# Holding back and interleaving PSUM drains in a two-layer attention kernel

## The chip, the cores and the metric

The kernel runs on one core of one Trainium2 chip. The metric is the device time of one execution in microseconds (us), less is better. The engines are called PE (TensorE, matrix products into PSUM), DVE (VectorE), ACT (ScalarE), POOL (GpSimd) and SP (SyncE, whose queue issues the DMAs).

## What is computed

Two attention layers, one after the other, on eight independent images (elements) of 512 channels and 32 x 32 = 1024 positions, all in fp32:

```python
# layer 0 (8 heads of 64 channels)
hn = group_norm(x, gn1_scale, gn1_bias)                     # 32 groups
q, k, v = split(einsum('bchw,oc->bohw', hn, w_qkv) + b_qkv) # per head
wgt = softmax(einsum('bct,bcs->bts', q * s, k * s))
a = einsum('bts,bcs->bct', wgt, v)
out = einsum('bchw,oc->bohw', a, w_proj) + b_proj
x = x + group_norm(out, gn2_scale, gn2_bias)
# layer 1 (one head of 512 channels; the rows of w_qkv, w_out are weight-normed)
qkv = einsum('oc,bcn->bon', w_qkv, x);  qkv = qkv / rms(qkv)
attn = softmax(einsum('bci,bcj->bij', q, k) * C ** -0.5)
h = einsum('oc,bcn->bon', w_out, einsum('bij,bcj->bci', attn, v))
x = (x + h) * 2 ** -0.5
```

## The kernel before

**Order.** Every instruction is issued through `InOrder` (line 34 is its call, so the profile names line 34 for nearly everything, and tiles tell the work apart). Each engine runs its instructions in program order; waits between engines are semaphores that the framework sets from the tiles' readers and writers. The order is written out by hand: generators (`steps`, `pieces`) issue a little work at each `next`.

**An element's layer 0** is a loop of 64 steps (`Heads.step`, 606): scores for 128 rows and two heads (`s`), softmax with its maximum on DVE (`nm`), exponential on ACT, scaling on POOL (`p<-p,tt`), a DVE transpose (`pb<-p`) in `turn` (560), four DMAs that lay the result out (`pT<-pb`), and for every second step 32 matmul passes with the values (`po<-pT,v`, `values`, 585). In the last eight steps POOL also forms the sums of the next element's input that the next stage needs (`tv`, lines 1242 on, one sum a step).

**Products in sevens.** `Seven` (715) computes a product of 2 x 2 blocks with seven products instead of eight. Their operands on one side are called B11, T2, T3, T4, T1, B22, B21, in this order; T1 to T4 are sums of blocks (`RightSide`, 678). Each product is two matmuls, which the trace shows as four passes. Two successive products share one PSUM tile (`product`, 730), whose name ends in B or T after its first product. A product's result is added into the outputs by small functions, the *drains*: `c11_first` (a copy on ACT), then sums on DVE (T2's into c12, T3's into c22, `c21`, `both` with two sums, `c12`, `c11`). They are put in a list, and the whole list is issued as soon as a tile has both its products (`Seven.drain`, 749). The tiles come from a pool of three (`wide`, 110; `ps_s`), which the scores share; a fourth tile waits until the first one is emptied.

**The hand-over from layer 0 to layer 1** (from line 1251, seven times: the last element has another ending, `finish_last`, 647). PE's work, in order:

- four products of the next element's values (`project_v7`, 517; profile names `p_v_B`, `p_v_T`). There are four units of seven products, 28 in all, one unit after the other;
- `values` for the last group but one (1255); then `heads.turn()` (1256) issues the last transpose and its DMAs; SP fetches the output projection's weights (`proj7`, profile name `proj`) and layer 1's norm matrix (`gram`);
- DVE forms five sums of the attention's output (`ta`), PE computes ten more products of the values;
- `values` for the last group (1271); the loads of `x`, for which a slot must be free, are queued on SP;
- `finish_layer0` (799): two units of seven products for the output projection (`p_o_B`, `p_o_T`) into `o`, whose statistics DVE takes (`bn_stats`, `bn_aggr`). Then the last fourteen products of the values are spread over the second group norm: four; `norm.means()` (PE's `pm`, then on DVE the mean, and `d`); two; `norm.coeffs()` (PE's `pv`, then `ve`, a Newton iteration for the inverse root in `rsqrt_steps`, 195, and the coefficients `a` and `c`); then four times two products, ACT's `o<-o,c,a` and DVE's `x<-x,o` for one of the four channel blocks;
- `Layer1.project` (865): `py`, the product of `x` with `gram`. The tile for channel block cj needs `x` up to block cj. DVE multiplies it with `x` and forms the sums `t` for the following sevens.

Of the kernel before, what the change touches and what calls it, by code (L numbers as in the profile page):

```python
# [10 lines left out]
AF = mybir.ActivationFunctionType  # L11
ALU = mybir.AluOpType
# [40 lines left out]
def attention_blocks_kernel(  # L53
# [29 lines left out]
    CI, NT, HN = C // P, N // P, N // 2  # L83
# [20 lines left out]
    PE, VE, AC, PO, SY = (InOrder(tc, e) for e in (nc.tensor, nc.vector, nc.scalar, nc.gpsimd, nc.sync))  # L104

    def big(name, lead=CI):

        return slots.take([P, lead, CI * N // lead], name)

    def wide(name):  # L110
        return ps_s.tile([P, 2, HN], F32, tag="sc", name=name)
# [11 lines left out]
    def run(pieces):  # L123
        for _ in pieces:
            pass
# [24 lines left out]
    def load_x(b, xt, ci):  # L150
        SY.dma_start(out=xt[:, ci, :], in_=xv[b, :, ci, :])
# [40 lines left out]
    def col(base, i):  # L192
        return cols[:, base + i : base + i + 1]

    def rsqrt_steps(r, v, n, name):

        t = small.tile([P, 4 * CI], F32, tag="rs_t", name=f"rs_{name}")[:, :n]
        VE.tensor_scalar(r.bitcast(I32), v.bitcast(I32), -0.5, 1597463007.0, ALU.mult, ALU.add)
        yield
        for _ in range(3):  # L200
            VE.tensor_mul(t, r, v)
            VE.tensor_mul(t, t, r)
            VE.tensor_scalar(t, t, -0.5, 1.5, ALU.mult, ALU.add)
            VE.tensor_mul(r, r, t)
            yield

    def rsqrt(r, v, n, name):
# [22 lines left out]
    def place(name, b):  # L230
        tag, shape = places[name]
        near[name] = weights.tile(shape, F32, tag=f"w_{tag}", name=f"{name}_{b}")
        if name == "v":

            near["v7"] = near[name]
            flat = near[name].rearrange("p k h c -> p (k h c)")
            near["v#"], near["v_"] = flat[:, CI * C :], flat[:, : CI * C]
            near[name] = flat[:, : CI * C].rearrange("p (ci c) -> p ci c", ci=CI)
        return near[name]
# [13 lines left out]
    def fetch(name, b):  # L253
        SY.dma_start(out=place(name, b), in_=far[name])
# [16 lines left out]
    def gn_stats(st, src, k):  # L271
        VE.bn_stats(st[:, k, :], src[:, k * HN : (k + 1) * HN])

    class GroupNorm:
# [8 lines left out]
        def mean_steps(self):  # L283
            mv, n = self.mv, self.n
            pm = self.bank(f"pm_{self.name}")
            PE.matmul(pm[:, :n], gavg, mv[:, :, 0], start=True, stop=True)
            yield

            self.mean, self.d = self.new("mean"), self.new("d")
            VE.tensor_copy(self.mean, pm[:, :n])  # L290
            VE.tensor_sub(self.d, mv[:, :, 0], self.mean)
            VE.tensor_mul(self.d, self.d, self.d)
            VE.tensor_add(self.d, self.d, mv[:, :, 1])

        def means(self):
            run(self.mean_steps())
# [121 lines left out]
    class Sums:  # L418
# [32 lines left out]
        def right(self, half, n, k):  # L451

            rows = halves[half]
            if n == 0 or (n, half) in ((1, 0), (3, 1)):
                return self.hn[rows, k, HN:] if n == 0 else self.hn[rows, k, :HN]
            return (self.t24 if n + half == 2 else self.t3)[rows, k]
# [60 lines left out]
    def project_v7(b, right, v):  # L517

        w = near["v7"]
        for m in range(CI):  # L520
            c = {f"{i + 1}{th + 1}": v[:, m + 4 * th, i * CH : (i + 1) * CH] for i in range(2) for th in range(2)}
            yield from Seven(
                f"v0_{b}_{m}", CH,
                lambda k, h: w[:, k, h, :], right(slice(m * P, (m + 1) * P)), c, lambda which: None, swap=True,
            ).steps()

    class Heads:
        def __init__(self, b, hn, v, qk):
# [186 lines left out]
    class Seven:  # L715
# [5 lines left out]

        half, drains = None, []

        def __init__(self, name, width, left, right, c, last, swap=False, bias=None):
            self.name, self.width, self.left, self.right, self.swap = name, width, left, right, swap
# [2 lines left out]
        def product(self, a, b, drain):  # L730
            first = Seven.half is None
            if first:
                tile_ = wide(f"p7_{self.name}_{b}")
                pm, Seven.half = tile_[:, 0], tile_[:, 1]
            else:
                pm, Seven.half = Seven.half, None
            pm = pm[:, : self.width]
            for h in range(2):
                l, r = self.left(a, h), self.right(b, h)
                if self.swap:  # L740
                    l, r = r, l
                PE.matmul(pm, l, r, start=(h == 0), stop=(h == 1))

            Seven.drains.append(lambda: drain(pm))
            if not first:
                Seven.drain()

        @staticmethod
        def drain():
            for f in Seven.drains:  # L750
                f()
            Seven.drains = []

        def steps(self):
            c, add, last = self.c, VE.tensor_add, self.last
# [43 lines left out]
    def finish_layer0(b, h, rhs, xt, v0):  # L799

        o, w = big(f"o_{b}"), near["proj7"]
        st = small.tile([P, CI, 2, 6], F32, tag="gn_st2", name=f"st2_{b}")
        mv = small.tile([P, CI, 2], F32, tag="gn_mv2", name=f"mv2_{b}")
        norm = GroupNorm(mv, CI, G2S, G2B, f"2_{b}")

        def unit(m):
            c = {
                f"{i + 1}{th + 1}": o[:, m + 2 * i, th * HN : (th + 1) * HN] for i in range(2) for th in range(2)
            }
            return Seven(  # L810
                f"o_{b}_{m}", HN,
                lambda k, hh: w[:, k, hh, m * P : (m + 1) * P], rhs.columns(slice(0, HN)), c, lambda which: None,
                bias=(col(BP, m), bpd[:, m : m + 1]),
            ).steps()

        def stats(j):
            for k in range(2):
                gn_stats(st[:, j], o[:, j, :], k)

        units = [unit(m) for m in range(2)]  # L820
        for u in units:
            next(u)

        for j in range(CI // 2 + 1, CI):
            rhs.sums(j)
        for m, u in enumerate(units):
            for k in range(6):
                next(u)
                if k == 3:
                    stats(m + 2)  # L830
            stats(m)
        slots.give(f"a_{b}")
        slots.give(f"ta_{b}")
        fetch("score", b)

        def products(n):
            for _ in range(n):
                next(v0)

        for j in range(CI):  # L840
            VE.bn_aggr(mv[:, j, :], st[:, j])
        products(4)
        norm.means()
        products(2)
        a, c = norm.coeffs()
        for j in range(CI):
            products(2)
            AC.activation(o[:, j, :], o[:, j, :], AF.Identity, bias=c[:, j : j + 1], scale=a[:, j : j + 1])
            VE.tensor_add(xt[:, j, :], xt[:, j, :], o[:, j, :])
        run(v0)  # L850
        slots.give(f"tv_{b + 1}")
        slots.give(f"o_{b}")

    class Layer1:
# [163 lines left out]
        def products(self, th, c, between=None):  # L1018
            self.po = bank(f"po1_{self.b}_{th}_{c}")
            e = self.e[th]  # L1020

            terms = [(self.v[:, t, c * P : (c + 1) * P], e[:, t, :]) for t in (0, 4, 1, 5, 2, 6, 7, 3)]
            for k, _ in enumerate(matmuls(self.po, terms)):
                if k == 1 and between:
                    between()
# [16 lines left out]
    gram = place("gram", 0)  # L1042
# [64 lines left out]
    coeffs = norm1.gn.all_steps()  # L1107
# [64 lines left out]
    for b in range(B):  # L1172
        hn, more = heads.hn, b + 1 < B
        todo, due, rest = iter(()), [], []
        for i in range(STEPS):
            j, r = divmod(i, NB)
# [29 lines left out]
            if not b:  # L1206
# [10 lines left out]
                if k == 0:  # L1217
                    coeffs = norm1.gn.all_steps()
# [13 lines left out]
            m, odd = divmod(i - STEPS + NB, 2)  # L1232
# [11 lines left out]
            if not more and i == STEPS - 4:  # L1244
                xt = big(f"x_{b}")
# [4 lines left out]
        if more:  # L1250
            v0_next = big(f"v0_{b + 1}", NT)
            v0 = project_v7(b + 1, right_v.columns, v0_next)
            for _ in range(4):
                next(v0)
        heads.values(STEPS // RG - 2)
        heads.turn()
        if more:
            fetch("proj7", b)
            fetch("gram", b)
            ta = big(f"ta_{b}").rearrange("p (k i) (h n) -> p k i h n", k=2, h=2)  # L1260
            rhs = RightSide(heads.a, ta[:, 0], ta[:, 1])
            for j in range(CI // 2 + 1):
                rhs.sums(j)
            for _ in range(10):
                next(v0)
        else:
            fetch("score", b)
            begun = OutBegun(b, heads)
            for ci in (2, 3):
                load_x(b, xt, ci)  # L1270
        heads.values(STEPS // RG - 1)
        slots.give(f"v0_{b}")
        if more:
            xt = big(f"x_{b}")
            for ci in range(CI):
                load_x(b, xt, ci)
            finish_layer0(b, heads, rhs, xt, v0)
        else:
            finish_last(b, heads, xt, o_last, begun)
# [81 lines left out]
```

## Time and profile before

| | us |
|---|---|
| median of 3 runs | 3277.99 (3277.52 to 3279.08) |
| the profiled execution | 3280.76 |
| its span, first to last instruction | 3278.6 |
| PE busy | 3223.2 |
| DVE busy | 2304.4 |
| POOL busy | 1200.7 |
| ACT busy | 1046.7 |
| one hand-over, element 2: first of 28 products to first `py` | 1077.25 to 1137.97 |

The busy times are sums over all stages. PE's matmuls are pipelined and their ends are modelled: a 128 x 512 pass is listed with 592 ns and a 128 x 256 pass with 379 ns, while passes in a row start every 0.43 and 0.216 us. So a gap on PE is best read from starts. In the timeline a row is: start, duration, engine, line, operation, output<-inputs, shape, number of instructions merged, and in brackets the idle time before the row with what ended it. In a list of waits a row is: who waited, for whom, total us, how often, longest.

### The profile page before, as it was taken

Reading aid. Unit: us, or ns where it says so; the run is one execution under the profiler, and the core shown is the slowest. Engines: PE = TensorE matmul, PEld = TensorE weight load, DVE = VectorE, ACT = ScalarE, POOL = GpSimd, SP = SyncE. Lnnn points to the kernel's source line nnn. Section 1 sums busy time; section 2 is a strip of 40 time slices with the busy share of each in tenths; the row PEclk is TensorE's granted clock in tenths of the full one; section 3 lists DMA queues with packets and bytes.
Section 4 is the critical chain, followed back from the end, with each engine's and each line's share of the span. In section 5 each row is a group of like instructions: output and inputs, shape, how many; then the busy total and the mean of one; then the engine's idle time right before and its main releaser. Section 6 shows DMA issues by size and latency. Waiting matters only on the chain. (4 is left out here: it accounts for less than half of the span.)

```text
span 3278.6 us, 36790 instructions
## 1 busy us (share of the span) xinstructions
PE 3223.2 (98%) x13346; PEld 1661.9 (51%) x13346; DVE 2304.4 (70%) x3182; ACT 1046.7 (32%) x1813; POOL 1200.7 (37%) x1004
## 2 busy tenths in 40 slices
PE   8999999999999999999999999999999999999899
PEld 5455644455444554445544555445554456445354
DVE  5696667866678656886668866687667876568653
ACT  2453114521145111551215402254023531245210
POOL 1553124721257112670226603265023641246121
PEclk9999999999999999999999999999999999999899
DMA  6777215862168511783228822388224872158500
GB/s 199 212 202 205 74 48 154 221 186 58 48 180 229 167 42 54 201 230 133 52 77 211 213 108 52 101 213 244 71 57 109 216 213 74 23 153 212 180 7 26
DMA packets 231579, 447.34 MB, mean 136 GB/s; under 512 B 28996, under 2 KB 69480, under 8 KB 225512
## 3 DMA queue, kind: packets, MB, share of 16 engines
q1 hardware_dynamic: 231280, 444.97, 48.6%
q8 instruction: 107, 1.75, 0.2%
q14 instruction: 72, 0.59, 0.1%
q10 hardware_dynamic: 120, 0.02, 0.0%
HBM read 133.06 MB, written 29.52 MB: 50 GB/s over the span
## 5 line engine op out<-in xcount | busy, mean ns | idle before, releaser
L34 ACT ACTIVATE p<-s,nm 128x1024 f32<-128x1024 f32 x512 | 565.6, 1109 | 888.3 <-DVE nm L34 782.8
L34 POOL TENSOR_SCALAR p<-p,tt 128x1024 f32<-128x1024 f32 x512 | 566.0, 1118 | 754.3 <-DVE tt L34 750.4
L34 DVE TENSOR_REDUCE nm<-s 128x1 f32<-128x1024 f32 x512 | 601.7, 1216 | 151.4 <-PE s L34 151.0
L34 DVE STREAM_TRANSPOSE pb<-p 128x2048 f32<-128x2048 f32 x256 | 589.8, 2304 | 36.1 <-DMA pT<-pb 27.2
L34 PE MATMUL s<-qk 64*128 64x512 f32 x2048 | 527.6, 604 | 1.4 <-POOL qk L34 0.8
L34 PE MATMUL po<-pT,v 128*64 128x256 f32 x4096 | 471.8, 383 | 3.0 <-DMA pT<-pb 2.9
L34 PE MATMUL po<-e,v 128*128 128x512 f32 x1024 | 451.7, 595 | 0.0
L34 PEld LDWEIGHTS po<-pT,v 128*64 128x64 f32 x4096 | 284.6, 137 | 221.4 <-ACT v L34 31.8
L34 POOL TENSOR_TENSOR u<-u,xy 128x512 f32<-128x512 f32 x64 | 78.9, 1270 | 764.5 <-DVE u L34 392.3
L34 PEld LDWEIGHTS s<-qk 64*128 64x128 f32 x2048 | 201.9, 186 | 252.1 <-issue 225.2
L34 PEld LDWEIGHTS po<-e,v 128*128 128x128 f32 x1024 | 191.9, 190 | 245.0 <-issue 236.4
L34 PE MATMUL pq<-hn,qk 64*128 64x512 f32 x504 | 197.1, 592 | 0.0
L34 POOL TENSOR_TENSOR esum<-esum,e 128x512 f32<-128x512 f32 x96 | 130.5, 1361 | 154.2 <-ACT e L34 151.7
L34 ACT ACTIVATE e<-e,shift,rinv 128x512 f32<-128x512 f32 x128 | 101.0, 812 | 256.6 <-DVE e L34 256.6
L34 DVE TENSOR_TENSOR v<-v,p_v_T 128x256 f32<-128x256 f32 x300 | 120.5, 418 | 84.4 <-PE p_v_T L34 80.3
L34 DVE TENSOR_TENSOR e<-e,p_e_T 128x512 f32<-128x512 f32 x160 | 106.9, 685 | 86.5 <-PE p_e_T L34 84.3
L34 PE MATMUL py<-x,gram 128*128 128x512 f32 x320 | 144.2, 607 | 16.2 <-DVE v L34 10.2
L34 PE MATMUL pqk<-hn,qk 64*128 64x512 f32 (+1 forms) x672 | 158.7, 590 | 0.0
L34 PE MATMUL pq<-t,qk 64*128 64x512 f32 x336 | 150.9, 589 | 0.0
L34 PE MATMUL pq<-v,qk 64*128 64x512 f32 x336 | 150.9, 589 | 0.0
L34 PE MATMUL p_e_T<-s,t 128*128 128x512 f32 x320 | 147.8, 592 | 0.0
L34 POOL TENSOR_TENSOR qk<-qk,v 128x512 f32<-128x512 f32 x96 | 127.0, 1332 | 3.2 <-ACT v L34 1.6
(221 smaller groups left out, 4041.6 us busy)
## 6 DMA issues: line engine op xcount, KB each, us to landing
pT<-pb SPq DMA_DIRECT2D x1024, 256.0 KB, 4.5
qk<-far_qk SPq DMA_DIRECT2D x21, 896.0 KB, 8.9
hn<-in_x_dram SPq DMA_DIRECT2D x32, 512.0 KB, 6.6
x<-in_x_dram SPq DMA_DIRECT2D x32, 512.0 KB, 6.9
out_dram<-x SPq DMA_DIRECT2D x32, 512.0 KB, 3.7
score<-far_score SPq DMA_DIRECT2D x8, 1792.0 KB
value<-far_value SPq DMA_DIRECT2D x8, 1792.0 KB, 7.2
proj<-far_proj SPq DMA_DIRECT2D x7, 1792.0 KB
```

What stands on the lines that cost most here:

```text
L34: return lambda *args, **kw: self._pin(call(*args, **kw))
```

## The change

- `rsqrt_steps`: a Newton step is r(1.5 - 0.5 r r v), now in three DVE operations and not four: t = (-0.5 r) r, t = t v, r = (t + 1.5) r. It is used by the weight norms at the start, by both group norms and by layer 1's root mean square.
- `mean_steps`: `d` is formed from PSUM directly; the copy of the mean comes after it.
- `project_v7`: the four units go in two pairs, and the two of a pair take turns, product by product. A pair of products in one tile is now the same product of two units.
- `Seven.hold()` keeps finished tiles from being drained, until `Seven.drain()`; `Seven.drain(n)` issues the n oldest drains alone.
- In the hand-over, the first four products are held over `values` and `heads.turn()` and drained after these. The fetch of `gram` goes from behind `proj7` to behind the loads of `x`.
- In `finish_layer0` the last fourteen products are held and drained piece by piece between the parts of the norm. Three of the four sums `x<-x,o` go from DVE to POOL, and all four ACT operations `o<-o,c,a` are issued in a row.

```diff
@@ rsqrt_steps
-            VE.tensor_mul(t, r, v)
-            VE.tensor_mul(t, t, r)
-            VE.tensor_scalar(t, t, -0.5, 1.5, ALU.mult, ALU.add)
-            VE.tensor_mul(r, r, t)
+            VE.scalar_tensor_tensor(t, r, -0.5, r, ALU.mult, ALU.mult)
+            VE.tensor_mul(t, t, v)
+            VE.scalar_tensor_tensor(r, t, 1.5, r, ALU.add, ALU.mult)
             yield
@@ mean_steps
-            VE.tensor_copy(self.mean, pm[:, :n])
-            VE.tensor_sub(self.d, mv[:, :, 0], self.mean)
+            VE.tensor_sub(self.d, mv[:, :, 0], pm[:, :n])
             VE.tensor_mul(self.d, self.d, self.d)
             VE.tensor_add(self.d, self.d, mv[:, :, 1])
+            VE.tensor_copy(self.mean, pm[:, :n])
@@ project_v7
-        for m in range(CI):
+
+        def unit(m):
             c = {f"{i + 1}{th + 1}": v[:, m + 4 * th, i * CH : (i + 1) * CH] for i in range(2) for th in range(2)}
-            yield from Seven(
+            return Seven(
...
+        for m in (0, 2):
+            units = [unit(m), unit(m + 1)]
+            for _ in range(7):
+                for u in units:
+                    next(u)
+                    yield
@@ Seven
-        half, drains = None, []
+        half, drains, held = None, [], False
...
-            if not first:
+            if not first and not Seven.held:
                 Seven.drain()
...
         @staticmethod
-        def drain():
-            for f in Seven.drains:
+        def hold():
+
+            Seven.held = True
+
+        @staticmethod
+        def drain(n=None):
+            for f in Seven.drains[:n]:
                 f()
-            Seven.drains = []
+            Seven.drains = [] if n is None else Seven.drains[n:]
+            if n is None:
+                Seven.held = False
@@ finish_layer0
+
+        Seven.hold()
         products(4)
+        Seven.drain(3)
         norm.means()
+        products(1)
+        Seven.drain(1)
+        coeffs = norm.coeff_steps()
+        next(coeffs)
+        products(3)
+        run(coeffs)
+        for j in range(CI):
+            AC.activation(
+                o[:, j, :], o[:, j, :], AF.Identity, bias=norm.c[:, j : j + 1], scale=norm.a[:, j : j + 1]
+            )
+        Seven.drain(2)
+        for j in range(CI):
+            (PO if j else VE).tensor_add(xt[:, j, :], xt[:, j, :], o[:, j, :])
         products(2)
-        a, c = norm.coeffs()
-        for j in range(CI):
-            products(2)
-            AC.activation(o[:, j, :], o[:, j, :], AF.Identity, bias=c[:, j : j + 1], scale=a[:, j : j + 1])
-            VE.tensor_add(xt[:, j, :], xt[:, j, :], o[:, j, :])
+        Seven.drain(2)
+        products(2)
+        Seven.drain(2)
+        products(2)
+        Seven.drain()
         run(v0)
@@ the hand-over
             v0 = project_v7(b + 1, right_v.columns, v0_next)
+            Seven.hold()
             for _ in range(4):
                 next(v0)
         heads.values(STEPS // RG - 2)
         heads.turn()
         if more:
+            Seven.drain()
             fetch("proj7", b)
-            fetch("gram", b)
...
             for ci in range(CI):
                 load_x(b, xt, ci)
+            fetch("gram", b)
             finish_layer0(b, heads, rhs, xt, v0)
```

## The prediction, made before the change was run

> **What bounds the kernel now.** I read the page's busy line first, then who waited for whom on the tensor engine (PE), then the timeline of one hand-over from an element's layer 0 to its layer 1 (element 2; the other six look the same to 0.02 us, except where a DMA is waited for).
>
> ```profile
> PE 3223.2 (98%) x13346; PEld 1661.9 (51%) x13346; DVE 2304.4 (70%) x3182; ACT 1046.7 (32%) x1813; POOL 1200.7 (37%) x1004
> ```
>
> PE is the bound. Work that moves on another engine is worth only the PE idle time that it removes, and all of that reaches the end, since PE has no slack elsewhere. Who PE waits for (total us, times, longest):
>
> ```profile
> PE py L34 <- DVE v L34: 10.2, 14, 1.2
> PE p_v_T L34 <- POOL tv L34: 8.5, 6, 1.4
> ...
> PE p_o_B L34 <- DMA proj<-far_proj: 5.3, 7, 1.4
> ...
> PE p_v_T L34 <- DMA pT<-pb: 1.4, 1, 1.4
> ```
>
> Three waits at each of seven hand-overs. The fourth line is the seventh of the second kind under another name (same place, same 1.42 us). The timeline of the first two (start, duration, engine, passes):
>
> ```profile
> 1079.08 1.46 PE L34 MATMUL p_v_T<-v,tv 128*128 128x256 f32 x6
> ...
> 1080.64 1.26 POOL L34 TENSOR_TENSOR tv<-hn,tv 128x512 f32<-128x512 f32 x1
> 1081.96 0.70 PE L34 MATMUL p_v_T<-v,tv 128*128 128x256 f32 x2 [1.42 <-POOL tv L34]
> ...
> 1082.59 3.67 PE L34 MATMUL po<-pT,v 128*64 128x256 f32 x32
> ...
> 1083.49 2.30 DVE L34 STREAM_TRANSPOSE pb<-p 128x2048 f32<-128x2048 f32 x1
> ...
> 1095.02 3.67 PE L34 MATMUL po<-pT,v 128*64 128x256 f32 x32
> ...
> 1099.84 3.67 PE L34 MATMUL p_o_B<-a,proj 128*128 128x512 f32 x8 [1.14 <-DMA proj<-far_proj]
> ```
>
> The fourth product waits for GpSimd's (POOL's) last sum, and later the output projection for its weights. The third wait:
>
> ```profile
> 1130.67 0.15 DVE L34 TENSOR_SCALAR ve<-pv 128x4 f32<-128x4 f32 x1
> ...
> 1133.83 0.16 DVE L34 TENSOR_TENSOR c<-cols,c 128x4 f32<-128x4 f32 x1
> ...
> 1134.63 4.63 ACT L34 ACTIVATE o<-o,c,a 128x1024 f32<-128x1024 f32 x4
> 1134.78 1.99 PE L34 MATMUL p_v_B<-v,hn 128*128 128x256 f32 x8
> ...
> 1135.90 1.22 DVE L34 TENSOR_TENSOR x<-x,o 128x1024 f32<-128x1024 f32 x1 [1.58 <-ACT o L34]
> ...
> 1137.04 0.87 DVE L34 TENSOR_TENSOR v<-v,p_v_T 128x256 f32<-128x256 f32 x2
> ...
> 1137.97 1.98 PE L34 MATMUL py<-x,gram 128*128 128x512 f32 x4 [1.19 <-DVE v L34]
> 1140.22 4.99 PE L34 MATMUL py<-x,gram 128*128 128x512 f32 x11 [0.27 <-DVE v L34]
> ```
>
> `py` starts when VectorE (DVE) has emptied a PSUM tile, and that emptying stands behind the norm's chain (1130.67 to 1133.99) and the first `x` sum.
>
> **True sizes.** Ends are modelled, so I count from starts. A 256-wide pass takes 0.216 us (x16 at 1131.31, next at 1134.78), a product is four: 0.865. A 512-wide pass takes 0.43. Wait 1: six passes from 1079.08 end at 1080.38; the next starts at 1081.96: 1.58. Wait 2: `po` to the next group is 3.60 undisturbed (1082.59 to 1086.19) and 4.82 here: 1.22, shown as 1.14; so the seven are 5.3 + 7 x 0.08 = 5.9, a mean of 0.84. Wait 3: eight passes from 1134.78 end at 1136.51, so 1.46 until 1137.97, then 0.54 more before 1140.22 (four passes of 0.43 end at 1139.68): 2.00. Per hand-over 1.58 + 0.84 + 2.00 = 4.42, in all 31 us: what there is to win.
>
> **What the Trainium skill says.** "Perfetto Trace Analysis", Identifying Performance Opportunities: a bubble that repeats on the engine that should be saturated can mean too few buffers in SBUF or PSUM for the next tile. The 14 `py` waits agree. "SBUF — State Buffer", Who interferes with whom: a DVE instruction with two SBUF inputs and a GpSimd instruction that reads SBUF exclude each other for a whole instruction; with one SBUF input they don't. The trace agrees: in the prologue the DVE sums `done<-done,done` (128x512) take 2986 ns beside POOL work, elsewhere such sums 685. "DMA: Bandwidth & Descriptors", Issuing engines are not separate DMA queues: all transfers share the 16 engines and interleave. The trace agrees: from 1090 to 1100 us the engines are 0.90 to 1.02 busy, at 244 to 409 GB/s, with `proj` (1.83 MB) and `gram` (1.05 MB) in flight together.
>
> **Part A, first ten products and the weights.** With the two units taking turns, the first four products are B11, B11, T2, T2. The last POOL sum makes T4, which is now seventh. T2's second half was summed at 1069.97. So wait 1 goes: `po` starts at 1081.0. The four drains are held, so the last DVE transpose, before queued behind them (1083.49), starts when POOL's scaling ends, 1080.67: 2.7 us earlier. Its four DMAs and then `proj` on SP's queue follow at once, so `proj` is issued at 1086.5 and not 1089.2. `gram` is now behind it and behind the `x` loads: 1.05 MB at some 0.35 MB/us, 3 us, leaves `proj`'s way. PE wants `proj` at 1097.4; with the latest landing (before: 1.41 us late) it is there with 3 us to spare, and still just in time if moving `gram` gives nothing. Wait 2 goes. `gram`, issued some 8 us later, after the `x` loads at 1097 to 1099, has until 1137; on SP it waits with the `x` loads for their slot, and nothing but `score` (issued at 1124) is queued behind it.
>
> New there: the held drains. Two of three PSUM tiles are full; ScalarE (ACT) empties the first behind `a<-po` (1084.72 + 0.47 + two copies of 0.37: 1085.9), in time for the tile wanted at 1086.4. DVE, whose adds wait for these copies with the `ta` sums queued behind, then does two adds (0.40 each, to 1086.4), five `ta` sums at 0.605 (to 1089.4) and two adds for T3 (1090.2). PE wants that tile for the sixth pair at 1084.6 + 6 x 0.865 + 0.1 = 1089.9: a new wait of 0.38. Later tiles are empty in time. A saves 1.58 - 0.38 + 0.84 = 2.04.
>
> **Part B, the last fourteen products.** Clock as if nothing earlier had moved (first product 1123.94). Four products end at 1127.40, where `pm` runs. Before, three DVE adds stood ahead of `mean` (1128.39), three more ahead of `ve` (1130.67). Now one add stands before (1127.6 to 1128.0; a tile is drained only when both its halves are done, as `v<-p_v_B` at 1125.87 shows), then three operations at 0.20 give `d` at 1128.6, `pv` follows with a PE wait of 0.2, the mean's copy and one add run beside it to 1129.2, and `ve` begins at 1129.25. The chain has 14 instructions and not 17, at 0.197 (3.32/17): 2.76, so `c` at 1132.0, 2.0 us earlier. `scalar_tensor_tensor` at 128x4 is not in the trace. At 128x512 it takes 692 to 751 ns, `tensor_tensor` 684. Bounds at 128x4: 0.16 to 0.23 us, a chain of 2.76 to 3.2 us; less than 0.16 is excluded, since every two-input row at 128x4 is 0.16 (159 to 163 ns), where the fixed part is all. I take 0.16.
>
> ACT makes `o0` by 1133.3, meanwhile DVE empties T3's tile (1132.8), then adds `x0` (1133.3 to 1134.45), then T4's tile (1135.25). PE wants that one for B21 at 1134.85: a wait of 0.4. B21 ends at 1137.0; S1's tile for `py` is emptied by then (four adds, to 1136.85), so `py` starts at 1137.05. Before, its effective start was 1137.97 + 0.54 = 1138.51. B saves 1.46.
>
> The `x1` to `x3` sums move to POOL, idle from 1081.9 to 1180.1. A 128x1024 sum isn't in the trace: two of 128x512 take 2.49, half of a 64x2048 one 2.25. I take 2.5, as upper bound. They end at 1137, 1139.5, 1142; PE wants them at 1138.8, 1142.2, 1149.9. They may block DVE's `t` sums (two SBUF inputs) until 1142, which PE's tile for the fourth `py`, wanted at 1147.3, covers. Cost nothing.
>
> **Elsewhere.** Start: PE's first `pG` (9.70) waits for a DVE chain with three operations fewer: 0.55, and PE is gapless after. End: in the last element the chain from `mean` to `c` stands open before `py` (3098.47): 3 x 0.2 + the copy 0.2 = 0.8. Other Newton chains lie beside PE work.
>
> **Sum.** 7 x (2.04 + 1.46) + 0.55 + 0.8 = 25.9. The profiled execution took 3280.76 us (span 3278.6); 3254.9 after. It lay 2.8 above the median of the runs, 3277.99, so 3252.
>
> **Rivals.** (1) *The new PSUM waits are longer*, and one part gives its gain back: the three-tile ring speaks for it, my margins of 0.2 to 0.5 us too. Without B: 7 x 2.04 + 1.35 = 15.6, 3262; if wait 1 only changes its place: 7 x (0.84 + 1.46) + 1.35 = 17.5, 3260. (2) *No new waits at all*: 4.42 x 7 + 1.35 = 32, 3246. (3) *Both parts give all back*: about 3277; speaks against it that the waits removed are in different places from the drains' chain. (4) *Slower: POOL's sums become PE's wait in `py`.* `x2` is due at 1134.45 + 2d, wanted at 1142.2: a wait of 2d - 7.75. It eats the 3.5 us saved when d passes 5.6 us a sum. At 7.5 us it is 7.25, a loss of 3.75 per hand-over, 26 - 1.35 = 25 us: 3303. The port lock speaks for it, the rows of 1.27 us per 512 against.
>
> **Chances.** Forecast (3249 to 3257) 0.58; (1) 0.20; (2) 0.14; (3) 0.04; (4) 0.04. Range 3244 to 3264: the forecast, most of (1) and (2). About 0.2% is what a measurement of this kernel can tell from no change (6.6 us): faster 0.92, same 0.04, slower 0.04.
>
> **What would show it.** `p_v_T <- POOL tv` and `p_o_B <- DMA proj` gone from PE's waits; the transpose right after POOL's scaling; a new short PE wait for DVE `v` in the ten products and before B21; `c` about 8.0 us after the second half's first product (10.05 before), `py` 13.1 after it (14.0 before, with a second gap). Wrong if `proj` still is waited for, if waits for DVE `v` sum to over 1.5 us per hand-over, or if PE waits for a POOL `x`.

## The result and the profile after

The changed kernel takes 3248.68 us in the median of 4 runs (3247.64 to 3249.94), the kernel before, beside it, 3277.76 (3277.39 to 3279.08). The ratio is 0.9911, with a 95% interval of 0.9894 to 0.9928. The profiled execution took 3249.17 us (span 3246.7), that of before 3280.76. So 31.6 us went between the profiled executions and 29.1 between the medians; 25.9 was forecast. The time lies between the forecast (3252) and the rival without new waits (3246).

The busy line of the page after:

```profile
PE 3217.5 (99%) x13346; PEld 1657.8 (51%) x13346; DVE 2274.4 (70%) x3074; ACT 1045.7 (32%) x1813; POOL 1253.0 (39%) x1025
```

PE does the same 13346 matmuls and is as busy as before within 6 us: most of the gain is idle time removed. DVE has 108 instructions fewer; 21 of them are the `x` sums, three at each of seven hand-overs, which POOL has more. PE's waits after (who waited for whom, total us, times, longest):

```profile
PE py L34 <- issue: 5.4, 1, 5.4
PE pG L34 <- DVE w_qk L34: 4.9, 1, 4.9
...
PE po L34 <- DMA pT<-pb: 3.4, 3, 2.8
...
PE p_o_B L34 <- DMA proj<-far_proj: 0.2, 1, 0.2
```

The three waits of the hand-over (10.2, 8.5 and 5.3 us in all) are gone but for 0.2 in one of seven. What is left lies at the start (`pG`), in the last element (`py`, `pm`, `pv`), and in the attention. The first half of element 2's hand-over, PE's timeline:

```profile
1067.79 1.99 PE L34 MATMUL p_v_B<-v,hn 128*128 128x256 f32 x8
1069.62 1.89 PE L34 MATMUL p_v_T<-v,tv 128*128 128x256 f32 x8
1071.44 3.67 PE L34 MATMUL po<-pT,v 128*64 128x256 f32 x32
...
1084.06 3.67 PE L34 MATMUL po<-pT,v 128*64 128x256 f32 x32
...
1087.98 3.67 PE L34 MATMUL p_o_B<-a,proj 128*128 128x512 f32 x8 [0.24 <-DMA proj<-far_proj]
```

`po` now starts 3.65 us after the first product (5.34 before): no product waits for POOL. The ten products take 12.62 from `po` to `po` (12.43 before): that is the new wait for a tile, 0.19. DVE and SP beside it (SPq is an issue on SP's DMA queue):

```profile
1071.25 2.31 DVE L34 STREAM_TRANSPOSE pb<-p 128x2048 f32<-128x2048 f32 x1 [2.35 <-POOL p L34]
...
1075.93 0.75 DVE L34 TENSOR_TENSOR v<-v,p_v_T 128x256 f32<-128x256 f32 x2 [2.37 <-ACT v L34]
...
1077.15 1.30 SPq L34 DMA_DIRECT2D proj<-far_proj  x1
...
1079.61 2.73 DVE L34 TENSOR_TENSOR v<-v,p_v_T 128x256 f32<-128x256 f32 x8
```

The transpose waits for POOL's scaling alone, and the held sums come behind it. The second half, from the first of the last fourteen products (1112.09):

```profile
1117.23 0.16 DVE L34 TENSOR_SCALAR ve<-pv 128x4 f32<-128x4 f32 x1
...
1117.63 0.16 DVE L34 SCALAR_TENSOR_TENSOR rs<-a 128x4 f32<-128x4 f32 x1
...
1119.79 0.16 DVE L34 TENSOR_TENSOR c<-cols,c 128x4 f32<-128x4 f32 x1
...
1121.26 1.23 DVE L34 TENSOR_TENSOR x<-x,o 128x1024 f32<-128x1024 f32 x1 [0.65 <-ACT o L34]
...
1122.41 2.06 DVE L34 TENSOR_TENSOR v<-v,p_v_T 128x256 f32<-128x256 f32 x6
1122.44 7.44 POOL L34 TENSOR_TENSOR x<-x,o 128x1024 f32<-128x1024 f32 x3 [49.98 <-ACT o L34]
...
1125.04 17.33 PE L34 MATMUL py<-x,gram 128*128 128x512 f32 x40
```

The chain ends 7.86 us after the half's start (10.05 before), `py` starts at 12.95 (14.03) and runs through: 17.33 for 40 passes is 40 x 0.43. POOL needs 2.48 us per `x` sum and PE waits for none.

Counted from starts, means of the seven hand-overs:

| us | first product to `po` | ten products, `po` to `po` | `po` to `p_o_B` | last fourteen products to `py` |
|---|---|---|---|---|
| before | 5.34 | 12.43 | 4.43 | 14.03, and 0.64 more within `py` |
| predicted | 3.76 | 12.81 | 3.59 | 13.1 |
| after | 3.66 | 12.62 | 3.67 | 12.95 |

The 40 passes of `py` take 17.81 us to the next product before and 17.17 after, hence the 0.64. The stretch between the third and the fourth column is 24.11 before and 24.13 after. So a hand-over saves 1.68 - 0.19 + 0.76 + 1.08 + 0.64 - 0.02 = 3.95, seven save 27.6. The first `p_v_B` of all comes 1.97 earlier (283.61 to 281.64), and in the last element `pm` to `py` is 0.75 shorter and the 40 passes of `py` take 18.88 and not 20.28. That makes 31.7 of the 31.9 between the two spans. What lies outside the hand-overs differs from execution to execution, as the part on the prediction shows.

### The profile page after: what moved, and what is told of

Its sections match the earlier page's. It is cut to its first block, busy times and chain, and to the rows that moved or that the text cites. A ratio compares the mean times of both kernels' runs of the same rounds, so it can differ in the third digit from the quotient of the medians.

```text
span 3246.7 us, 36723 instructions
## 1 busy us (share of the span) xinstructions
PE 3217.5 (99%) x13346; PEld 1657.8 (51%) x13346; DVE 2274.4 (70%) x3074; ACT 1045.7 (32%) x1813; POOL 1253.0 (39%) x1025
## 4 chain that ended last, share of the span: by engine, by line
PE 93%; DMA 3%; DVE 2%; SPq 1%; issue 1%; POOL 0%; DVEq 0%
PE po L34 26%; PE s L34 13%; PE pq L34 7%; PE p_e_T L34 7%; PE p_v_T L34 6%; PE p_e_B L34 5%; PE p_v_B L34 5%; PE py L34 4%; PE pqk L34 4%; PE p_u_T L34 3%; PE p_o_T L34 3%; DMA pT<-pb 3%; PE p_u_B L34 3%; PE p_o_B L34 2%; SPq L34 1%; DVE pb L34 1%
## 5 line engine op out<-in xcount | busy, mean ns | idle before, releaser
L34 POOL TENSOR_TENSOR x<-x,o 128x1024 f32<-128x1024 f32 x21 | 52.1, 2512 | 348.3 <-ACT o L34 348.3
```

Source lines behind the costliest of these rows:

```text
L34: return lambda *args, **kw: self._pin(call(*args, **kw))
```

## Experiments

The theory is that of the prediction: turn-taking removes the wait for POOL, holding lets the transpose and `proj` go earlier, piecewise draining with the shorter chain frees `py`. The rivals are that one of these parts does all of it, or that what covers the parts costed at nothing is thin. Each kernel was timed beside the kernel before (medians 3278.53 in the first four, 3277.49 in the next four, 3279.03 in the last three). Unless said otherwise, an edit is made to the changed kernel. The intervals reach some 5 us to either side (2 where 14 or 20 runs were taken), so what an edit of 3 to 5 us does is read from starts in the traces, and the medians alone do not show it.

**The fetch of `gram` back to its place behind `proj`** (e1), and ahead of it (e2).

```diff
             fetch("proj7", b)
+            fetch("gram", b)
...
-            fetch("gram", b)
             finish_layer0(b, heads, rhs, xt, v0)
```

> The changed kernel, with the fetch of gram put back directly behind proj7 on SP's queue. Theory now: transfers of one queue are served in order, so one that is issued later takes nothing from an earlier one; proj came in time because it was issued 2.7 us earlier, and the move of gram did nothing. Expected: 3248.7, within 1.5 us; PE's wait for proj stays at some 0.2 us in all. Rival, the step of the prediction: proj and gram share the engines, and gram costs proj 3 us. Then PE waits for proj again, 0.5 to 3 us at each of seven hand-overs: 3252 to 3268.

> The changed kernel, with gram fetched directly ahead of proj7. In-order theory: gram's 1.05 MB go first, at some 0.35 MB/us, so proj lands about 3 us later; it had been wanted just when it came in one hand-over (0.24 us of wait), and up to about 1 us after it had come in the others: PE waits for proj 2 to 3 us at each, in all 14 to 21, 3263 to 3270. Sharing theory: about the same as with gram behind proj7, since both are in flight together either way, within 3 us of that run.

With `gram` behind: 3247.37 us (3246.6 to 3254.2), ratio 0.9913 (0.9899 to 0.9928), as fast as the change. With `gram` ahead: 3260.8 (3256.3 to 3266.9), ratio 0.9949 (0.9932 to 0.9966), 12 us worse. In the traces' DMA packets `proj` is 128 packets of 14336 bytes. Its last packet ends so long after its issue, as a mean of the seven hand-overs: 9.55 us in the kernel before (which has `gram` behind too), 9.67 in the changed kernel, 9.99 with `gram` behind, 10.82 with `gram` ahead. PE's only wait for it with `gram` behind (0.2 was expected, as in the change):

```profile
PE p_o_B L34 <- DMA proj<-far_proj: 0.9, 1, 0.9
```

In these means a transfer behind `proj` on SP's queue delays it by 0.3 us, or not at all (9.55 before); one ahead of it costs 1.2 us of landing, and 1.2 us more because `proj` itself is issued later (6.73 us after `po`, 5.57 in the change). PE's waits with `gram` ahead:

```profile
PE p_o_B L34 <- DMA proj<-far_proj: 8.5, 5, 2.2
...
PE p_o_B L34 <- DVE ta L34: 3.9, 2, 2.5
```

`p_o_B` reads `a` and `proj` and no `ta`, and these two waits too end 11 to 12 us after the issue of `proj`: both rows are waits for `proj`. All seven hand-overs wait, 12.4 us in sum, and two of the waits (2.5 and 2.2 us) are followed by half clock on PE, another 3 us. So moving `gram` gained nothing; what removed the wait is the earlier issue of `proj`, 5.57 us after `po` and not 6.79.

**No holding in the first half** (e3).

```diff
             v0 = project_v7(b + 1, right_v.columns, v0_next)
-            Seven.hold()
             for _ in range(4):
```

> The changed kernel without the hold over values and the last transpose: the first two tiles are drained as soon as they are full. Theory: the turn-taking alone removes the wait for POOL's last sum; the hold keeps two DVE adds (0.75 us, ready only at 1072.3 on the changed kernel's clock) from standing ahead of the last transpose (1071.25). Without it the transpose, its DMAs and proj come some 1.0 us later, so PE waits for proj up to 1.0 us more per hand-over, and the wait of 0.19 us for a tile in the ten products goes: between 1 us faster and 6 us slower than 3248.7, likeliest 3252. Rival: the hold is what removes the wait for POOL. Then 1.6 us per hand-over come back: 3260.

3252.05 us (3250.6 to 3254.0), ratio 0.9923 (0.9909 to 0.9938): 3.4 slower than the change.

```profile
PE p_o_B L34 <- DMA proj<-far_proj: 5.2, 6, 1.4
```

The wait for `proj` is back and the wait for a tile is gone (12.43 from `po` to `po`). Holding is worth the difference of the two, as the prediction set them against each other: 0.74 - 0.18 per hand-over, 3.9 us in all.

**Units one after the other again, all else of the change kept** (e4).

```diff
-        def unit(m):
+        for m in range(CI):
...
-            return Seven(
+            yield from Seven(
...
-        for m in (0, 2):
-            units = [unit(m), unit(m + 1)]
-            for _ in range(7):
-                for u in units:
-                    next(u)
-                    yield
```

> The changed kernel with the units of the values' products one after the other again (all else as changed). Theory: the fourth product is T4 again and waits for POOL's last sum, 1.6 to 1.7 us at each of seven hand-overs, 11 to 12 us; in the norm's stage tiles hold two different products and DVE's sums depend on each other (0.40 us apart and not 0.33), 0 to 3 us in all: 3260 to 3264. Rival: the gain of the first part is the hold's, which lets the transpose go first, and turn-taking matters little: 3249 to 3252.

3280.14 us (3277.5 to 3284.5), ratio 1.0006 (0.9999 to 1.0012): a miss of 16 us and more, the whole gain is gone. PE's waits:

```profile
PE p_v_B L34 <- ACT v L34: 11.1, 7, 1.6
PE p_v_T L34 <- POOL tv L34: 10.0, 7, 1.4
PE p_v_T L34 <- DVE v L34: 7.1, 7, 1.0
```

Only the second line, the wait for POOL, was expected. The first, in element 2's second half:

```profile
1129.70 4.63 ACT L34 ACTIVATE o<-o,c,a 128x1024 f32<-128x1024 f32 x4 [5.53 <-DVE c L34]
...
1134.24 0.35 ACT L34 COPY v<-p_v_B 128x256 f32<-128x256 f32 x1
...
1134.64 1.99 PE L34 MATMUL p_v_B<-v,hn 128*128 128x256 f32 x8 [1.58 <-ACT v L34]
```

One by one, a new unit begins in the middle of the half, and its first drain is a copy on ACT; issued behind the four operations `o<-o,c,a`, it keeps a tile full and PE waits. With two units in turn both copies fall ahead of the norm. The third line is a tile of the ten products, whose sums stand behind the `ta` sums on DVE. Counted from starts the ten take 13.72, a wait of 1.29, where turn-taking leaves 0.19. So the holds and the counted drains rely on turn-taking: it decides which drains come when, and on which engine. I had costed it for the wait for POOL alone.

**Turn-taking alone, put into the kernel before** (e9, the reverse of e4).

> The kernel before with one edit alone: the two units of a pair take turns. Theory: it brings most of what the whole change brings. The wait for POOL's last sum goes (1.69 us per hand-over); the wait for proj stays (0.8), since the transpose stands behind two DVE sums; in the norm's stage the drains of a tile are of one kind, so less DVE work stands ahead of the chain: about 0.7 us. 2.4 us at each of seven hand-overs, 17: 3261 (3257 to 3264). Rival: turn-taking pays only with the holds and the new order of the norm's stage: 3266 (the first wait alone, 12 us) or slower.

3259.46 us (3258.5 to 3263.0), ratio 0.9946 (0.9929 to 0.9962): 19.6 us of the gain from this one edit. PE's waits that remain:

```profile
PE py L34 <- DVE v L34: 5.8, 7, 0.8
PE p_o_B L34 <- DMA proj<-far_proj: 4.9, 6, 1.5
```

The first `py` of element 2's hand-over:

```profile
1129.72 17.52 PE L34 MATMUL py<-x,gram 128*128 128x512 f32 x40 [0.83 <-DVE v L34]
```

First product to `po` takes 3.66, as in the change. It also shortens the wait of `py`: the second half takes 13.52 (14.03 before), the gap of 0.8 included, and `py` then loses 0.18 and not 0.64. From starts the seven hand-overs are 17.5 us shorter.

**The norm's stage in its old order** (e5): `products`, `norm.means()`, `norm.coeffs()` and the `x` sums on DVE as before; turn-taking, holding in the first half and the shorter chain kept.

```diff
-        Seven.hold()
         products(4)
-        Seven.drain(3)
         norm.means()
...
+        products(2)
+        a, c = norm.coeffs()
         for j in range(CI):
-            (PO if j else VE).tensor_add(xt[:, j, :], xt[:, j, :], o[:, j, :])
...
+            products(2)
+            AC.activation(o[:, j, :], o[:, j, :], AF.Identity, bias=c[:, j : j + 1], scale=a[:, j : j + 1])
+            VE.tensor_add(xt[:, j, :], xt[:, j, :], o[:, j, :])
```

> The changed kernel with the norm's stage as before: drains as soon as a tile is full, two products between the parts, the four sums of x on DVE in the loop (units taking turns, three-operation Newton steps and the first part's hold stay). Theory: the reordering of the second part brought 1.62 us per hand-over less 0.6 that the shorter Newton chain brings by itself; some 0.7 to 1.2 us come back at each of seven: 3254 to 3257. Rival: the second part's gain is the Newton chain's alone: 3248 to 3250.

3252.09 us (3249.4 to 3254.0), ratio 0.9925 (0.991 to 0.9939): less is lost than expected.

```profile
PE py L34 <- DVE v L34: 1.4, 7, 0.2
PE p_o_B L34 <- DVE ta L34: 1.3, 1, 1.3
```

The half takes 12.90 to `py` and 0.18 more within it, against 12.95: the reordering itself, with its POOL sums, is worth 0.13 us per hand-over, 1 us in all. The medians stand 3.4 apart, which their intervals don't tell from 1; the second row, a late `proj` in one hand-over, is part of it, and the rest stays open.

**Newton's step in four operations** (e6).

```diff
-            VE.scalar_tensor_tensor(t, r, -0.5, r, ALU.mult, ALU.mult)
-            VE.tensor_mul(t, t, v)
-            VE.scalar_tensor_tensor(r, t, 1.5, r, ALU.add, ALU.mult)
+            VE.tensor_mul(t, r, v)
+            VE.tensor_mul(t, t, r)
+            VE.tensor_scalar(t, t, -0.5, 1.5, ALU.mult, ALU.add)
+            VE.tensor_mul(r, r, t)
```

> The changed kernel with Newton steps of four operations again. Theory: the chain to c is 0.6 us longer in every hand-over, and with it x0, the emptying of T4's tile, and the last pair of products: about 0.5 us each, 3.5; 0.5 at the start, 0.6 at the end: 3252 to 3254. Rival: the chain is hidden behind the products now, only start and end count: 3249.5 to 3250.5.

3254.14 us (3252.9 to 3254.4), ratio 0.9931 (0.9916 to 0.9946), 5.5 slower.

```profile
PE p_v_B L34 <- DVE v L34: 3.4, 7, 0.5
```

The half takes 13.57, 0.62 more (4.3 us in all), for three operations more at 0.2. The chain lies wholly on PE's path even in the new order.

**All `x` sums on DVE** (e7), and **the work of POOL doubled** (e8: another sum, of two blocks of `o`, ahead of each; nothing reads what it writes).

```diff
-            (PO if j else VE).tensor_add(xt[:, j, :], xt[:, j, :], o[:, j, :])
+            VE.tensor_add(xt[:, j, :], xt[:, j, :], o[:, j, :])
```

```diff
         for j in range(CI):
+            if j:
+                PO.tensor_add(o[:, j - 1, :], o[:, j - 1, :], o[:, j, :])
             (PO if j else VE).tensor_add(xt[:, j, :], xt[:, j, :], o[:, j, :])
```

> The changed kernel with all four sums x<-x,o on DVE, in the new order. Theory: x1 to x3 (1.14 us apart, each waiting for its ACT operation) stand ahead of the emptying of T4's tile, so the last pair of products starts 3.3 us later at each hand-over; nothing is won back: 22 us, 3271. Rival: POOL was not needed, PE hardly sees it: under 3253.

> The changed kernel, with a second POOL sum of the same size (into blocks of o that are no longer used, nothing of the result depends on it) ahead of each of the three, so that each x block takes POOL about 5.0 us and not 2.5. It tests the price in the slow rival of the prediction, a wait of 2d - 7.75 for x2. By it 2.2 us of PE wait per hand-over, 15 us: 3264 (3261 to 3267). If the cover is larger than I worked out, under 3255; if the port lock between POOL and DVE adds to it, over 3270.

POOL doubled: 3257.69 us (3256.4 to 3261.2), ratio 0.9944 (0.9929 to 0.9959).

```profile
PE py L34 <- POOL x L34: 6.0, 7, 0.9
```

```profile
1125.66 7.03 PE L34 MATMUL py<-x,gram 128*128 128x512 f32 x16
...
1133.54 6.73 PE L34 MATMUL py<-x,gram 128*128 128x512 f32 x15 [0.84 <-POOL x L34]
```

The rival's mechanism is real, and in the change its cover holds. The two pairs of sums up to `x2` took 2.37 + 2.34 + 2.69 + 2.80 = 10.2 us. By the prediction's 2d - 7.75 PE would wait 2.45; it waited 0.84. PE first reads `x2` after 16 passes of `py`, as the row shows, where I had counted the 12 of the first two tiles (for `x3` I did count the passes within its tile): 4 x 0.43 = 1.7 us more cover.

All on DVE: 3285.51 us (3279.4 to 3291.0), ratio 1.0023 (1.0014 to 1.0031), 14 us more than expected, although the wait is what was worked out:

```profile
PE p_v_B L34 <- DVE v L34: 22.9, 7, 3.3
```

The windows behind it (from:to in us, their length, then busy us and number of instructions of PE, PEld, DVE, ACT and POOL, PE's granted clock, DMA share, GB/s):

```profile
1130.00:1132.00 2.00, 1.01 (x5) 0.56 (x3) 2.00 (x3) 2.00 (x3) 0.00 (x0) 1.00 0.00 0
1132.00:1134.00 2.00, 0.00 (x0) 0.00 (x0) 2.00 (x4) 0.30 (x1) 0.00 (x0) 0.79 0.00 0
1134.00:1136.00 2.00, 1.72 (x4) 1.45 (x5) 2.00 (x7) 0.00 (x0) 0.00 (x0) 0.50 0.04 8
...
1138.00:1140.00 2.00, 2.00 (x4) 0.87 (x3) 1.35 (x3) 0.00 (x0) 0.00 (x0) 0.50 0.49 115
1140.00:1142.00 2.00, 2.00 (x6) 0.83 (x5) 1.16 (x2) 0.00 (x0) 0.00 (x0) 1.00 0.97 373
```

PE is idle from 1131.01 to 1134.28. A mean of 0.79 over 2 us is 0.84 us at one half, so the half clock lasts from 1133.16 to 1140.0, 6.84 us, of which PE works in 5.7. It comes, for 3.4 or 6.8 us, in six of the seven hand-overs. Against the one hand-over without it (16.36 us to `py`, then 17.17), the other six lose 12.3 us in sum. The next kernel tests whether that is the rest of the loss.

**All `x` sums on DVE, with PE kept busy in the gap** (e11): 14 matmuls of 128 columns into a tile that nobody reads.

```diff
+    def busy(n):
+        t = bank("busy")
+        for _ in range(n):
+            PE.matmul(t[:, :P], ident, ones, start=True, stop=True)
...
         Seven.drain(2)
+        busy(14)
         products(2)
```

> The run with all four sums of x on DVE again, with 14 small matmuls whose result nobody reads in the 3.3 us in which PE waits ahead of the last pair of products. The wait stays. Theory: the 14 us by which that run exceeded what its waits explain are half-clock windows that follow these waits; with PE busy there they go: 3271 (3268 to 3274). Rival: they came from elsewhere: 3283 to 3288.

3272.44 us (3269.1 to 3277.3), ratio 0.9978 (0.9971 to 0.9984), 13 us better than e7. Two windows of 4 us at the same place:

```profile
1130.00:1134.00 4.00, 3.85 (x22) 3.05 (x21) 3.90 (x11) 0.00 (x0) 0.00 (x0) 1.00 0.00 0
1134.00:1138.00 4.00, 4.00 (x11) 1.77 (x10) 2.60 (x4) 0.00 (x0) 0.00 (x0) 1.00 0.91 315
```

The clock stays at 1.00 and the time is within 1.5 us of what was worked out for e7 itself (3271), so the rest of e7's loss was half clock after the gap. That DVE makes the last pair of products 3.3 us late holds: the half takes 16.36, with the unread matmuls in the gap, and not 12.95.

**Unread matmuls at the start and in the last element** (e10): the same function, with 5 and 10 around the first transpose on PE, 16 ahead of the last element's `pm` and 18 behind its `pv`.

> The changed kernel, with small matmuls whose result nobody reads where PE is idle before the first weights and in the last element's norm (5 and 10, and 16 and 18, of 128x128). It leaves nothing out. Theory: after some microseconds of idle PE runs at half clock for whole windows of 3.41 us; kept busy it starts the first pG and the last py at full clock: up to 1.7 us at the start, 1.5 at the end, 3245.5 (3244.5 to 3247.5). Rival: these matmuls stand in the way of the real ones and give the gain back: 3249 or more.

3245.5 us (3243.8 to 3246.4), ratio 0.9901 (0.9886 to 0.9915), the fastest of all; 3.2 better than the change, with intervals that overlap. The last element's `py` in the change, and then here:

```profile
3067.91 18.88 PE L34 MATMUL py<-x,gram 128*128 128x512 f32 x40 [5.39 <-issue]
```

```profile
3060.93 4.26 PE L34 MATMUL busy<-ones,ident 128*128 128x128 f32 x36
3066.43 17.43 PE L34 MATMUL py<-x,gram 128*128 128x512 f32 x40 [1.23 <-DVE x L34]
```

The passes run at full clock from the first. At the start `pG` also runs faster (17.53, not 19.17 us), but it begins at 10.88 and not 9.20, and the next stage (`pcol`) at 36.97 against 36.94. In the eight other traces with the start of the change it begins at 37.26 to 38.35, so whether something was gained there too stays open.

## Why the prediction was right, and where its sizes were off

- **Wait for POOL: right.** 1.68 us removed per hand-over, 1.58 forecast. That it goes by turn-taking alone is shown by e9 and e4.
- **New wait for a held tile: right in place, half the size.** 0.19, 0.38 forecast (its own times, 1090.2 against 1089.9, give 0.3). DVE's first held sums began 4.49 us after `po` (4.6 forecast), the `ta` sums at 5.16 (5.4), and T3's tile was empty at 8.92 (9.2), when PE had wanted it at 8.8 (8.9). A copy on ACT that comes earlier and sums that start 0.33 apart, not 0.40 (`x8` in 2.73), are the difference.
- **Wait for `proj`: right in the sum, wrong in one reason.** 0.76 removed, 0.84 forecast. Counted from the first product the transpose and `proj` did go some 2.7 us earlier; PE itself is 1.68 earlier by then, so from `po` it is 1.1 and 1.2 us. But the step "`gram` leaves `proj`'s way: there with 3 us to spare" failed: e1 shows that the move gives nothing, and the last packet of `proj` ends 9.67 us after its issue (9.55 before), 1.0 us before PE wants it and not 3. What held is the clause beside it, "still just in time if moving `gram` gives nothing". I had read the two transfers in flight together as sharing the engines. The Trainium skill, "DMA: Bandwidth & Descriptors", Queues, rings and completion order, says that on each engine descriptors are taken in the order of the ring; both fetches are on SP's queue, and e1 and e2 agree (9.99 with `gram` behind, 10.82 with it ahead). That section, and not the one on interleaving, bore on this step.
- **Second half: right, 1.72 for 1.46.** `ve` came at 5.14 (forecast 5.3), `c` ended at 7.86 (8.06), and T4's tile was empty at about 11.1 (11.3), so that the wait of 0.4 before B21 shrank to about 0.1. `scalar_tensor_tensor` at 128x4 takes 0.16 as chosen; the chain's pitch is 0.197 as before (3.16 us over 16 starts; the quotient written beside it, 3.32/17, is 0.195). What the part *does* was less well told: by e9, e5 and e6 the gain of this half comes from turn-taking and the shorter chain; the reorder and the POOL sums bring about 0.13 per hand-over.
- **POOL sums: right.** 2.48 each, 2.5 forecast. The lock that the Trainium skill describes in "SBUF — State Buffer", Who interferes with whom, shows: DVE's `t` sums of two SBUF inputs take 1.77 and 1.70 beside them and 0.68 afterwards, up to 2.83 with POOL doubled. PE waits for none of it. The rival lies further off than the prediction put it, by the 1.7 us that e8 showed.
- **Start and end: 1.35 forecast, about 4.1 in the two profiled executions, much of it chance.** I counted operations alone (0.55 + 0.8); `pG` does start 0.50 earlier, and at the end 0.75 went. Most of the rest is clock: from the first `pG` to `pcol` PE does the same work in 27.74 us (9.20 to 36.94) and not 28.80 (9.70 to 38.50), and the last element's `py` takes 18.88 and not 20.28. Both follow an idle stretch of PE of about 5 us. The Trainium skill, "TensorE: Matmul & The Clock Gate", What's actually happening, describes windows of some 3.4 us that run free of the kernel, with half clock after an idle one. The traces agree on the length (e7: 6.84 us, two such windows) and on the remedy (e10: full clock in `py` after matmuls in the gap), less on the condition: in e7 the clock fell 2.15 us after PE's last matmul. Where the windows lie differs from execution to execution. Eight more traces have the start and end of the change (e1 to e5, e7, e8, e11): there that first stretch takes 28.03 to 29.16 and `py`, counted to the next product, 18.77 to 20.19 (18.72 in the change), so the profile of the change caught the best case at both places. The means of these nine traces, against the three with the longer Newton step (before, e6, e9), give 0.8 at the start and 1.4 at the end, about 2.1.

By edits, from the medians: turn-taking 19.6 (e9), the shorter chain about 5.5 with start and end (e6), holding 3.4 (e3), the norm's order 1 to 3.4 (e5), moving `gram` nothing (e1). From starts, in the seven hand-overs alone: 17.5, 4.3, 3.9, 0.9 and nothing, 26.6 of the 27.6. This is no price list of independent parts: e9 adds its edit to the kernel before, the others take theirs out of the change, and taking turn-taking out costs 31.5 (e4). The forecast's two halves hid that: 2.04 and 1.46 per hand-over, each made of pieces that need the turn-taking.

## What to carry to other kernels

Before pieces of a drain are held or counted out, look at which engine each piece uses and what is queued on that engine by then: the same counts that fit one order of products cost all the gain in another. On a queue served in order only what stands ahead of a transfer delays it, so move the issue itself, not what follows it. When a gap on PE passes 2 us, price the half clock that can follow too; unread matmuls in the gap are a cheap way to see it, and sometimes to remove it. Where a profile holds such a gap, compare several executions before a difference of 1 or 2 us is explained.

## What had not been expected of the hardware

- An idle stretch of PE of 3.27 us was enough for half clock in six of seven hand-overs, and it fell when PE had been idle for 2.15 us in the one shown. It cost about 13 us in all (e7 against e11), some 2 us each.
- The 13 traces hold the clock's own record, and it gives a sharper rule than a length of gap. Within a trace all changes of the clock lie whole multiples of 3.413 us apart. Laid on that grid, with PE's ends as modelled, each of the 42 windows after which the clock fell has 2.04 us or more without a matmul, and no other window at full clock has more than 2.01. It rose again after windows with at most 0.46 us idle and stayed low after those with 0.60 or more. So a gap counts by its part in one window: the seventh gap of e7 was split into 1.61 and 1.65 us and cost nothing, and a gap of 2.17 us in e2, nearly all in one window, was followed by half clock.
- Successive DVE sums of 128x256 from PSUM start 0.33 us apart where they don't touch each other's data (`x8` in 2.73), and 0.45 where one uses or overwrites data of the one before (`x2` in 0.87); at 128x4 a copy between the chain's operations costs 0.08 and not 0.2. The prediction priced the sums at 0.40 and the copy at 0.2.
